# A graph-transformer layer on one core: one fp32 product fewer in front, lookup rows loaded by GpSimd, and the last messages moved ahead of the numerators and FFN transposes

## The chip, the cores and the metric

The kernel runs on one core of a Trainium2 chip. Its time is the device time in microseconds (us) of a whole launch; the median of several runs is compared. One further execution is profiled, and all durations of single instructions come from it. The engines are TensorE (PE, with its weight loads PEld), VectorE (DVE), ScalarE (ACT), GpSimd (POOL) and SyncE (SP). DMAs can be issued from SP, ACT and POOL.

## The reference

The input is a table `x` of N = 1250 nodes with D = 1024 features, and 20000 edges with source, destination and one of R = 8 relation types. With `xn = layernorm(x)`:

```
u   = xn @ root + bias + sum over r of mean over edges of type r into the node (xn[src]) @ weight[r]
z   = concat(u, xn) @ w_gate + b_gate
gnn = tanh(u) * z + xn * (1 - z)
mix = second-order Taylor linear attention of rms_norm(xn), 8 heads of 16, then @ w_out
x1  = x + gnn + mix
out = x1 + ffn(layernorm(x1))       # gate and up 1024 -> 352, silu, down 352 -> 1024,
                                    # weights and activations rounded to fp4 by blocks of 16
```

All inputs and outputs are float32.

## The kernel before, in words

Nodes are cut into ten blocks of up to 128 rows, and D into two column halves of 512. The kernel computes `y[r] = xn @ weight[r]` for all relations to DRAM (`y_d`, one array for each half), then gathers one row of it for every edge, weights it, and sums the rows by destination.

**Front.** LayerNorm (L186 to L200) takes each block: statistics on DVE, a square root on ACT, `normalize` (L125, L126) on DVE, a square with a sum on ACT (L194), eight transposes on PE (`transpose_cols`, L156), and two evacuations of the transposed tiles to `xnT`. `evac` (L84 to L90) gives evacuations in turn to ACT and DVE when `turns[0]` is 1, and to one engine alone when it is 0. Beside it a counting sort of the edges by destination runs: 16 steps build one-hot rows on DVE and counts on PE; tables are made of them; then 32 chunks of 5 x 125 edges (L307 to L336) look the tables up. A chunk loads the destinations of its 625 edges, the same row for all 128 partitions (`db`), takes the low seven bits (`lb`, L313), compares with the partition number (`lT`, L315, the weights of 20 small matmuls, L325 and L327), builds masks (L231), reduces the products (L328, L330), and counts equal destinations before each edge (`eq`, L333, five times). The pool of these tiles has two buffers. When all is known (L354), GpSimd scatters the 160 sorted columns of edge records to DRAM (`sort_d`, L363). PE's other work in the front is `plain(r)` (L369 to L390): fp32 products of half 0 for the first PLAIN = 4 relations, 80 matmuls of 128x128 by 128x512 each. Beside the last of them `x_limbs` (L403 to L416) splits `xnT` into three fp32r parts.

**Limb products.** The remaining products are made of three matmuls on the parts (L522 to L524): 240 matmuls for each. First come the R - PLAIN = 4 others of half 0, with 22 pieces of FFN weight quantisation on DVE spread among them (`ffn_rows`, to DRAM as `fgu_d` and `fdn_d`); then the eight of half 1, with the messages of half 0 among them; then five (queries and keys, root, gate of `x`) with 140 (EARLY) messages of half 1. A message (`gather` L437, `segments` L446 to L456) is 128 gathered rows, a selection matrix, two fp32r parts, two matmuls, a copy and a store to `seg_d`. LAG = 2 messages are gathered ahead, and GpSimd issues the gathers.

**Tail.** A list `rest` (L782 to L786) holds the attention sums, the preparation of open segments, `open_segments(0)`, ten `mix_pairs` (sums of key-value products), and FFN weight tiles to transpose (`ffn_weight`: load by SP, transposes, evacuations to `wguT` and `wdT`), with five numerators (`mix_num`, FIRST = 5) between them. The messages that are left, 19 calls, are spread over all of it but its last AFTER = 8 items. After the last message `open_segments(1)` (L756 to L771) loads the last row of each tile of `seg_d`, multiplies by selection matrices and adds the sums to `seg_d` by an indirect DMA from GpSimd (L769). SP loads the gate weights `wg` (4 MB) and `wo` at the end. Then ten blocks finish the layer (L810 to L892): a block gathers its segment sums (`ag`, L822), adds the root product to `u` (L828), transposes it, and makes the gate products (L836) and the FFN (L861, L877).

The order in which each engine carries out its instructions is fixed when the program is built, by a scheduler that knows the dependencies and estimates of durations; `issue_after` holds an instruction behind another one. A buffer of a pool is given again when its last reader is done, and memory of a closed pool is used again by later tiles, which then wait.

Of the kernel before, what the change touches and what calls it, by code (L numbers as in the profile page):

```python
# [8 lines left out]
F32 = mybir.dt.float32  # L9
F32R = mybir.dt.float32r  # L10
BF = mybir.dt.bfloat16
I32 = mybir.dt.int32
AF = mybir.ActivationFunctionType
ALU = mybir.AluOpType
# [4 lines left out]
N, D, R, E, I = 1250, 1024, 8, 20000, 352  # L19
NB, BR = 10, 128  # L20
KC = D // 128
# [4 lines left out]
MORE = 4096  # L26
H, DH = 8, 16
FIRST = 5
AFTER = 8
LAG = 2  # L30
EARLY = 140
PLAIN = 4
TOP = -4096
LOW = 2.0 ** -12
EXPONENT = 0x7F800000
# [13 lines left out]
def gps_layer(ctx: ExitStack, tc: tile.TileContext, x, src, dst, et, w_rel, w_root, bias,  # L49
# [19 lines left out]
    fgu_d = dram.tile([2 * I, D], F32, name="fgu_d")  # L69
    fdn_d = dram.tile([D, I], F32, name="fdn_d")  # L70
    seg_d = [dram.tile([ZERO + 1 + ST, HD], F32, name=f"seg{i}_d") for i in range(2)]
    sort_d = dram.tile([128 * ST, 4], F32, name="sort_d")

    def mm_tile():
# [10 lines left out]
    def evac(o, i):  # L85
# [3 lines left out]
        else:  # L89
# [8 lines left out]
    pidx = const.tile([128, 1], F32, name="pidx")  # L98
    G.iota(pidx, pattern=[[0, 1]], base=0, channel_multiplier=1,
           allow_small_or_imprecise_dtypes=True)  # L100
    eps = const.tile([128, 1], F32, name="eps")
    V.memset(eps, 1e-5)
    hdiff = const.tile([128, H], F32, name="hdiff")
# [21 lines left out]
    def normalize(o, xt, mr):  # L125
        V.tensor_scalar(o, xt, mr[:, 0:1], mr[:, 1:2], op0=ALU.subtract, op1=ALU.mult)  # L126
# [51 lines left out]
    with ExitStack() as front:  # L178
# [3 lines left out]
        xnT = xp.tile([128, KC, N], F32, name="xnT")  # L182


        with tc.tile_pool(name="ln", bufs=2) as ln:
            for b in range(NB):  # L186
                n = rows_of(b)
                xt = ln.tile([BR, D], F32, name="xt", bufs=8)[:n]
                nc.sync.dma_start(xt, x[block_rows(b), :])
                mr = stat[:n, b, :]  # L190
                mean_rstd(ln, mr, xt)
                normalize(xt, xt, mr)
                sq = ln.tile([BR, D], BF, name="sq", bufs=1)[:n]
                S.activation(sq, xt, AF.Square, accum_out=rms[:n, b, 0:1])  # L194
                transpose_cols(xnT, xt, n, D_CHUNKS, b * BR)
            V.tensor_scalar(rms[:, :, 0], rms[:, :, 0], 1e-24, None, op0=ALU.max)
            S.activation(rms[:, :, 0], rms[:, :, 0], AF.Sqrt)
            V.reciprocal(rms[:, :, 0], rms[:, :, 0])
            V.tensor_scalar(rms[:, :, 0], rms[:, :, 0], float(D) ** 0.5, None, op0=ALU.mult)
            V.tensor_scalar(rms[:, :, 1], rms[:, :, 0], float(DH) ** -0.5, None, op0=ALU.mult)  # L200


        with (tc.tile_pool(name="so", bufs=1, side="right") as so,
              tc.tile_pool(name="sc", bufs=2, side="right") as sc):
# [5 lines left out]
            hi_i = so.tile([80, 2, EP], I32, name="hi_i")  # L210
            V.tensor_scalar(lo_i, raw["dst"], 127, None, op0=ALU.bitwise_and)
            V.tensor_scalar(hi_i, raw["dst"], 7, None, op0=ALU.logical_shift_right)
            fl = so.tile([80, 5, 2, EP], F32, name="fl")
            V.tensor_copy(fl[:, 0], lo_i)
            V.tensor_copy(fl[:, 1], hi_i)
# [90 lines left out]
            LT = 5  # L306
            for c in range(ET // LT):  # L307
                t0 = c * LT
                db = sc.tile([128, LT * EP], I32, name="db")
                nc.sync.dma_start(db, bass.AP(tensor=dst.tensor, offset=dst.offset + t0 * EP,  # L310
                                              ap=[[0, 128], [1, LT * EP]]))
                lb = sc.tile([128, LT * EP], I32, name="lb")
                V.tensor_scalar(lb, db, 127, None, op0=ALU.bitwise_and)  # L313
                lT = sc.tile([128, LT * EP], BF, name="lT")
                V.tensor_scalar(lT, lb, pidx, None, op0=ALU.is_equal)  # L315
                msk = sc.tile([EP, LT, 2 * NHI + NHI * R], F32, name="msk")
# [336 lines left out]
    def mix_transposed(b):  # L653
        num = nums.pop(b)
        pt = tr_tile()
        n = rows_of(b)
        T.transpose(pt[:, 0, :n], num.rearrange("p h e -> p (h e)"), ident[:n, :n])
        S.copy(mixT[:, block_rows(b)], pt[:, 0, :n])

    with ExitStack() as late:  # L660
        op = late.enter_context(tc.tile_pool(name="op", bufs=1))
        pb = late.enter_context(tc.tile_pool(name="pb", bufs=8))
        kv = op.tile([BR, NB, 257], F32, name="kv")
        V.memset(kv[:, :, 256:257], 1.0)

# [105 lines left out]
                    in_=osum[:n, :], in_offset=None, compute_op=ALU.add)  # L771

        def ffn_weight(src, r0, n, c0, wide, o, chunks, col):
            wt = rawp.tile([128, HD], F32, name="raw")
            nc.sync.dma_start(wt[:n, :wide], src[r0:r0 + n, c0:c0 + wide])
            transpose_cols(o[:, c0 // 128:, :], wt, n, chunks, col)

# [1 line left out]
                   for i in range(2) for r0, n in I_CHUNKS for c0 in (0, HD)]  # L779
        down = [lambda a=(fdn_d, r0, n, 0, I, wdT, I_CHUNKS, r0): ffn_weight(*a) for r0, n in D_CHUNKS]  # L780
        rest = [mix_sums, open_rows, lambda: open_segments(0)]
        rest += [lambda b=b: mix_pairs(b) for b in range(NB)] + gate_up[:4]  # L782
        for b in range(FIRST):
            rest.append(lambda b=b: (mix_num(b), mix_transposed(b - 1) if b else None))
        rest += gate_up[4:] + down
        done = EARLY  # L786
        for i, p in enumerate(rest):
            p()
            while done < ST + LAG and (done - EARLY) * (len(rest) - AFTER) < (i + 1) * (ST + LAG - EARLY):
                message(1, done)  # L790
                done += 1
                if done == ST + LAG:
                    open_segments(1)
        for k in range(0, KC, 2):
            nc.sync.dma_start(wg[:, k:k + 2, :], w_gate[k * 128:(k + 2) * 128, :].rearrange("(k p) n -> p k n", p=128))
        nc.sync.dma_start(wo, w_out)
    late_r.close()
    mid.close()
# [121 lines left out]
```

## Time and profile before

| what | us |
|---|---|
| median of 3 runs (lowest, highest) | 2032.33 (2029.03, 2034.07) |
| the profiled execution, time | 2034.48 |
| the profiled execution, span of the core | 2032.7 |
| PE busy in the span | 1916.1 |
| DVE busy | 1319.7 |
| ACT busy | 736.0 |
| POOL busy | 569.5 |
| first limb product of half 0 starts | 352 |
| first gather of a message | 607 |
| last matmul of the last limb product ends | 1508.5 |

The mean TensorE clock granted in the span was 0.959 of full speed. In the profile a row of a group gives the line, the engine, the operation, the tiles with their shapes and the count, then busy time and mean nanoseconds of one, then the idle time of the engine just before and what ended it. A row of the timeline gives the start in us from the start of the span, the duration, the engine and the operation, and in brackets the idle time before it with what ended it. An fp32 matmul shows as two records, an fp32r one as one. The modelled end of a matmul can overlap the next one's start, so the count and the length of a full stretch tell more than the mean.

### The profile page before, as it was taken

How to read it: one execution, taken by the hardware profiler on the slowest of the kernel's cores; microseconds unless marked ns; L12 is line 12 of the kernel's file. 1: busy time of each engine (PE TensorE's matmuls, PEld its weight loads, DVE VectorE, ACT ScalarE, POOL GpSimd, SP SyncE). 2: the span in 40 equal slices, each digit the busy share in tenths (PEclk: the TensorE clock that was granted, in tenths of full speed). 3: DMA queues.
4: the chain of work that ended last, by engine and by line, in shares of the span. 5: the costliest groups of instructions: out<-in, count | busy, mean ns of one | idle time of the engine just before them, and what ended most of it. 6: DMA issues, size and time to landing. Idle time of an engine off the chain costs nothing. (4 is left out here: it accounts for less than half of the span.)

```text
span 2032.7 us, 23764 instructions
## 1 busy us (share of the span) xinstructions
PE 1916.1 (94%) x7748; PEld 1266.7 (62%) x7748; DVE 1319.7 (65%) x2947; ACT 736.0 (36%) x1279; POOL 569.5 (28%) x519
## 2 busy tenths in 40 slices
PE   8999999999999999999999989989889959999998
PEld 4465544777777777777777867767663324454544
DVE  9989840677765555455655675765667737777665
ACT  4111241111125554454554455555553123232311
POOL 1000177885003333233233234323234120010000
PEclk9999999999999999999999989999888559999999
DMA  5233222444337666667776678777788242122100
GB/s 207 70 109 121 86 68 51 132 120 125 121 127 240 223 223 222 221 221 230 228 224 208 204 248 258 243 237 252 235 285 314 76 137 85 63 83 68 37 21 29
DMA packets 159345, 327.81 MB, mean 161 GB/s; under 512 B 26414, under 2 KB 35284, under 8 KB 159222
## 3 DMA queue, kind: packets, MB, share of 16 engines
q10 hardware_dynamic: 76570, 141.23, 18.8%
q0 software_dynamic: 33952, 91.27, 17.3%
q1 hardware_dynamic: 48700, 93.79, 14.5%
q8 instruction: 61, 1.00, 0.2%
q14 instruction: 62, 0.51, 0.1%
HBM read 179.54 MB, written 146.49 MB: 160 GB/s over the span
## 5 line engine op out<-in xcount | busy, mean ns | idle before, releaser
L522 PE MATMUL ab<-wH,xH 128*128 128x512 f32 (+3 forms) x1360 | 536.9, 395 | 3.0 <-ACT wH L481 2.8
L524 PE MATMUL ab<-wD,xD 128*128 128x512 f32 (+3 forms) x1360 | 530.6, 396 | 6.1 <-DVE wD L483 5.6
L523 PE MATMUL ab<-wL,xL 128*128 128x512 f32 (+3 forms) x1360 | 533.3, 393 | 0.1
L437 POOL DMA_INDIRECT msg<-y_d,key x314 | 327.5, 1043 | 682.8 <-PE sm L454 402.1
L450 DVE SCALAR_TENSOR_TENSOR msg<-msg,weight,hi 128x512 fp32r<-128x512 f32 x314 | 234.1, 749 | 139.0 <-ACT hi L448 132.1
L524 PEld LDWEIGHTS ab<-wD,xD 128*128 128x128 f32 (+1 forms) x1360 | 253.2, 187 | 77.4 <-DVE wD L483 17.5
L522 PEld LDWEIGHTS ab<-wH,xH 128*128 128x128 f32 (+1 forms) x1360 | 255.3, 188 | 61.8 <-ACT wH L481 5.4
L523 PEld LDWEIGHTS ab<-wL,xL 128*128 128x128 f32 (+1 forms) x1360 | 254.8, 187 | 60.7 <-DVE wL L482 1.2
L381 PE MATMUL mm<-wt,xnT 128*128 128x512 f32 (+1 forms) x640 | 292.2, 601 | 0.0
L363 POOL DMA_INDIRECT sort_d<-pay,row x160 | 202.7, 1267 | 281.2 <-DVE pay L354 232.7
L448 ACT ACTIVATE hi<-msg,weight 128x512 fp32r<-128x512 f32 x314 | 221.8, 721 | 104.5 <-DMA msg<-y_d,key 38.5
L455 ACT COPY seg<-sm 128x512 f32<-128x512 f32 x314 | 181.7, 584 | 192.4 <-PE sm L454 157.7
L530 ACT ACTIVATE yt<-ab 128x512 f32<-128x512 f32 (+3 forms) x170 | 100.1, 592 | 272.2 <-PE ab L523 253.8
L531 DVE SCALAR_TENSOR_TENSOR yt<-ab,yt 128x512 f32<-128x512 f32 (+3 forms) x170 | 114.9, 679 | 124.7 <-ACT yt L530 119.5
L381 PEld LDWEIGHTS mm<-wt,xnT 128*128 128x128 f32 (+1 forms) x640 | 114.6, 188 | 119.8 <-issue 118.8
L446 DVE TENSOR_SCALAR sel<-iota_n,last_row 128x128 fp32r<-128x128 f32 x314 | 89.1, 286 | 108.5 <-PE sm L454 108.3
L453 PE MATMUL sm<-hi,sel 128*128 128x512 f32 x314 | 134.9, 433 | 25.9 <-ACT hi L448 19.6
L454 PE MATMUL sm<-msg,sel 128*128 128x512 f32 x314 | 137.0, 436 | 22.7 <-DVE msg L450 22.4
L836 PE MATMUL mm<-wg,uT 128*128 128x512 f32 (+1 forms) x320 | 142.5, 598 | 1.5 <-DVE mr L121 1.0
L482 DVE TENSOR_TENSOR wL<-raw,h 128x512 fp32r<-128x512 f32 x136 | 92.8, 682 | 70.9 <-PE mm L381 70.9
L481 ACT CAST wH<-h 128x512 fp32r<-128x512 f32 x136 | 83.6, 621 | 129.6 <-DVE h L480 117.2
L836 PEld LDWEIGHTS mm<-wg,uT 128*128 128x128 f32 (+1 forms) x320 | 59.9, 190 | 75.8 <-issue 71.2
(263 smaller groups left out, 2032.0 us busy)
## 6 DMA issues: line engine op xcount, KB each, us to landing
seg_d<-seg ACTq DMA_DIRECT2D x314, 256.0 KB
y_d<-yt ACTq DMA_DIRECT2D x144, 256.0 KB
raw<-in_L_gnn_weight_dram SPq DMA_DIRECT2D x96, 256.0 KB
db<-in_dst_dram SPq DMA_DIRECT2D x32, 312.5 KB
xt<-in_x_dram SPq DMA_DIRECT2D x18, 512.0 KB
wt<-in_L_gnn_weight_dram SPq DMA_DIRECT2D x24, 256.0 KB
msg<-y_d,key POOLq DMA_INDIRECT x314, 4.6
root_d<-yt ACTq DMA_DIRECT2D x18, 256.0 KB
```

The source lines that it names most:

```text
L363: st = G.indirect_dma_start(out=sort_d[:, :], out_offset=bass.IndirectOffsetOnAxis(ap=row[:, t:t + 1], axis=0), in_=pay[:, t, :], in_offse ...
L381: T.matmul(ps[:n], xnT[:, k, block_rows(b)], held[k], start=(k == 0), stop=(k == KC - 1))
L437: gathered_last[0] = G.indirect_dma_start(out=msg[:, :], out_offset=None, in_=y_d[nh][:, :], in_offset=bass.IndirectOffsetOnAxis(ap=key[:, ...
L448: S.mul(hi, msg, weight[:, t:t + 1])
L450: V.scalar_tensor_tensor(lo, msg, weight[:, t:t + 1], hi.bitcast(F32), op0=ALU.mult, op1=ALU.subtract)
L453: T.matmul(ps, sel, hi, start=True, stop=False)
L454: T.matmul(ps, sel, lo, start=False, stop=True)
L455: S.copy(seg, ps)
L522: T.matmul(pa[:p, :n], xH[:, k, ns], Wh[:, :n], start=(k == 0), stop=False)
L523: T.matmul(pa[:p, :n], xL[:, k, ns], Wl[:, :n], start=False, stop=(k == KC - 1))
L524: T.matmul(pb[:p, :n], xD[:, k, ns], Wd[:, :n], start=(k == 0), stop=(k == KC - 1))
L836: T.matmul(ps[:n], uT[:, k, :n], wg[:, k, cs], start=(k == 0), stop=(k == KC - 1))
```

## The change

1. PLAIN is 3 instead of 4: three fp32 products in front, five limb products of half 0 behind.
2. LayerNorm's normalisation goes to ACT (an Identity pass with a scale, and a bias `shift` that DVE makes, one column per block), and all LayerNorm evacuations go to ACT. After it evacuations alternate again.
3. The low bits of the destinations are written once to DRAM as bf16 (`lo_d`). Each lookup chunk loads `db` on 125 partitions instead of 128 and `lb` from `lo_d` on 128, both from GpSimd's queue; the DVE instruction that made `lb` is gone, and `lT` is made from bf16.
4. FFN weight tiles have a pool of their own with six buffers (`fw`) instead of the three of the limb weights.
5. All remaining messages are spread over the sums, open segments and pairs alone; `open_segments(1)` follows directly. Then come five numerators, each followed by four of the 20 FFN weight tiles.
6. GpSimd loads `wg`, held behind its last gather, instead of SP.

```diff
--- before.py
+++ after.py
@@ -26,10 +26,9 @@
 MORE = 4096
 H, DH = 8, 16
 FIRST = 5
-AFTER = 8
 LAG = 2
 EARLY = 140
-PLAIN = 4
+PLAIN = 3
 TOP = -4096
 LOW = 2.0 ** -12
 EXPONENT = 0x7F800000
@@ -69,6 +68,7 @@
     fgu_d = dram.tile([2 * I, D], F32, name="fgu_d")
     fdn_d = dram.tile([D, I], F32, name="fdn_d")
     seg_d = [dram.tile([ZERO + 1 + ST, HD], F32, name=f"seg{i}_d") for i in range(2)]
+    lo_d = dram.tile([1, E], BF, name="lo_d")
     sort_d = dram.tile([128 * ST, 4], F32, name="sort_d")
 
     def mm_tile():
@@ -98,6 +98,7 @@
     pidx = const.tile([128, 1], F32, name="pidx")
     G.iota(pidx, pattern=[[0, 1]], base=0, channel_multiplier=1,
            allow_small_or_imprecise_dtypes=True)
+    shift = const.tile([BR, NB], F32, name="shift")
     eps = const.tile([128, 1], F32, name="eps")
     V.memset(eps, 1e-5)
     hdiff = const.tile([128, H], F32, name="hdiff")
@@ -182,6 +183,7 @@
         xnT = xp.tile([128, KC, N], F32, name="xnT")
 
 
+        turn[0], turns[0] = 1, 0
         with tc.tile_pool(name="ln", bufs=2) as ln:
             for b in range(NB):
                 n = rows_of(b)
@@ -189,7 +191,8 @@
                 nc.sync.dma_start(xt, x[block_rows(b), :])
                 mr = stat[:n, b, :]
                 mean_rstd(ln, mr, xt)
-                normalize(xt, xt, mr)
+                V.scalar_tensor_tensor(shift[:n, b:b + 1], mr[:, 0:1], -1.0, mr[:, 1:2], op0=ALU.mult, op1=ALU.mult)
+                S.activation(xt, xt, AF.Identity, bias=shift[:n, b:b + 1], scale=mr[:, 1:2])
                 sq = ln.tile([BR, D], BF, name="sq", bufs=1)[:n]
                 S.activation(sq, xt, AF.Square, accum_out=rms[:n, b, 0:1])
                 transpose_cols(xnT, xt, n, D_CHUNKS, b * BR)
@@ -199,6 +202,7 @@
             V.tensor_scalar(rms[:, :, 0], rms[:, :, 0], float(D) ** 0.5, None, op0=ALU.mult)
             V.tensor_scalar(rms[:, :, 1], rms[:, :, 0], float(DH) ** -0.5, None, op0=ALU.mult)
 
+        turns[0] = 1
 
         with (tc.tile_pool(name="so", bufs=1, side="right") as so,
               tc.tile_pool(name="sc", bufs=2, side="right") as sc):
@@ -210,6 +214,9 @@
             hi_i = so.tile([80, 2, EP], I32, name="hi_i")
             V.tensor_scalar(lo_i, raw["dst"], 127, None, op0=ALU.bitwise_and)
             V.tensor_scalar(hi_i, raw["dst"], 7, None, op0=ALU.logical_shift_right)
+            lo_b = so.tile([80, 2, EP], BF, name="lo_b")
+            V.tensor_copy(lo_b, lo_i)
+            G.dma_start(lo_d.rearrange("o (a b c) -> b (o a) c", a=2, b=80), lo_b)
             fl = so.tile([80, 5, 2, EP], F32, name="fl")
             V.tensor_copy(fl[:, 0], lo_i)
             V.tensor_copy(fl[:, 1], hi_i)
@@ -306,11 +313,11 @@
             LT = 5
             for c in range(ET // LT):
                 t0 = c * LT
-                db = sc.tile([128, LT * EP], I32, name="db")
-                nc.sync.dma_start(db, bass.AP(tensor=dst.tensor, offset=dst.offset + t0 * EP,
-                                              ap=[[0, 128], [1, LT * EP]]))
-                lb = sc.tile([128, LT * EP], I32, name="lb")
-                V.tensor_scalar(lb, db, 127, None, op0=ALU.bitwise_and)
+                db = sc.tile([EP, LT * EP], I32, name="db")
+                G.dma_start(db, bass.AP(tensor=dst.tensor, offset=dst.offset + t0 * EP,
+                                       ap=[[0, EP], [1, LT * EP]]))
+                lb = sc.tile([128, LT * EP], BF, name="lb")
+                G.dma_start(lb, lo_d[:, t0 * EP:(t0 + LT) * EP].to_broadcast([128, LT * EP]))
                 lT = sc.tile([128, LT * EP], BF, name="lT")
                 V.tensor_scalar(lT, lb, pidx, None, op0=ALU.is_equal)
                 msk = sc.tile([EP, LT, 2 * NHI + NHI * R], F32, name="msk")
@@ -660,6 +667,7 @@
     with ExitStack() as late:
         op = late.enter_context(tc.tile_pool(name="op", bufs=1))
         pb = late.enter_context(tc.tile_pool(name="pb", bufs=8))
+        fw = late.enter_context(tc.tile_pool(name="fw", bufs=6))
         kv = op.tile([BR, NB, 257], F32, name="kv")
         V.memset(kv[:, :, 256:257], 1.0)
 
@@ -771,7 +779,7 @@
                     in_=osum[:n, :], in_offset=None, compute_op=ALU.add)
 
         def ffn_weight(src, r0, n, c0, wide, o, chunks, col):
-            wt = rawp.tile([128, HD], F32, name="raw")
+            wt = fw.tile([128, HD], F32, name="fw")
             nc.sync.dma_start(wt[:n, :wide], src[r0:r0 + n, c0:c0 + wide])
             transpose_cols(o[:, c0 // 128:, :], wt, n, chunks, col)
 
@@ -779,20 +787,25 @@
                    for i in range(2) for r0, n in I_CHUNKS for c0 in (0, HD)]
         down = [lambda a=(fdn_d, r0, n, 0, I, wdT, I_CHUNKS, r0): ffn_weight(*a) for r0, n in D_CHUNKS]
         rest = [mix_sums, open_rows, lambda: open_segments(0)]
-        rest += [lambda b=b: mix_pairs(b) for b in range(NB)] + gate_up[:4]
-        for b in range(FIRST):
-            rest.append(lambda b=b: (mix_num(b), mix_transposed(b - 1) if b else None))
-        rest += gate_up[4:] + down
+        rest += [lambda b=b: mix_pairs(b) for b in range(NB)]
         done = EARLY
         for i, p in enumerate(rest):
             p()
-            while done < ST + LAG and (done - EARLY) * (len(rest) - AFTER) < (i + 1) * (ST + LAG - EARLY):
+            while done < ST + LAG and (done - EARLY) * len(rest) < (i + 1) * (ST + LAG - EARLY):
                 message(1, done)
                 done += 1
-                if done == ST + LAG:
-                    open_segments(1)
-        for k in range(0, KC, 2):
-            nc.sync.dma_start(wg[:, k:k + 2, :], w_gate[k * 128:(k + 2) * 128, :].rearrange("(k p) n -> p k n", p=128))
+        open_segments(1)
+
+        with tc.issue_after(gathered_last[0]):
+            for k in range(0, KC, 2):
+                G.dma_start(wg[:, k:k + 2, :], w_gate[k * 128:(k + 2) * 128, :].rearrange("(k p) n -> p k n", p=128))
+        weights = gate_up + down
+        for b in range(FIRST):
+            mix_num(b)
+            if b:
+                mix_transposed(b - 1)
+            for p in weights[len(weights) * b // FIRST:len(weights) * (b + 1) // FIRST]:
+                p()
         nc.sync.dma_start(wo, w_out)
     late_r.close()
     mid.close()
```

## The prediction

> **What bounds the kernel now.** The sections with busy totals and with tenths of the span come first: TensorE is busy nearly everywhere, so only its thin places and its own work can give time.
>
> ```profile
> PE 1916.1 (94%) x7748; PEld 1266.7 (62%) x7748; DVE 1319.7 (65%) x2947; ACT 736.0 (36%) x1279; POOL 569.5 (28%) x519
> ...
> PE   8999999999999999999999989989889959999998
> PEclk9999999999999999999999989999888559999999
> ```
>
> The one thin place is slice 33 (a 5, with a granted clock of 5 in it and before it). Then I cut the span at the joints: end of the one-hots, end of the lookups, first limb product, first message, last limb matmul, last pair, last numerator, and the first transpose of `u` in the ten final blocks.
>
> ```profile
> 0.00:101.40 101.40, 91.46 (x566) 49.45 (x567) 94.49 (x260) 29.25 (x69) 7.79 (x20) 1.00 0.41 138
> 101.40:236.40 135.00, 133.52 (x860) 77.53 (x860) 121.04 (x506) 15.01 (x44) 0.00 (x0) 1.00 0.36 116
> 236.40:352.00 115.60, 114.42 (x269) 49.65 (x268) 41.59 (x95) 34.10 (x67) 87.01 (x72) 1.00 0.21 50
> 352.00:587.10 235.10, 228.33 (x960) 176.05 (x961) 162.70 (x331) 43.43 (x73) 115.69 (x89) 1.00 0.42 122
> 587.10:1508.70 921.60, 880.26 (x3695) 686.53 (x3694) 551.76 (x1097) 474.37 (x806) 296.47 (x292) 0.98 0.72 230
> 1508.70:1574.50 65.80, 54.84 (x194) 22.87 (x193) 48.22 (x115) 23.52 (x42) 29.20 (x18) 0.82 0.92 325
> 1574.50:1621.90 47.40, 45.47 (x82) 15.18 (x81) 34.66 (x82) 8.53 (x18) 5.70 (x6) 0.50 0.22 69
> 1621.90:1669.20 47.30, 21.34 (x84) 11.85 (x83) 17.35 (x46) 13.35 (x26) 8.99 (x7) 0.61 0.42 116
> 1669.20:2032.70 363.50, 346.43 (x1047) 177.57 (x1047) 247.85 (x420) 94.46 (x138) 18.61 (x16) 0.98 0.18 60
> ```
>
> After the times each line gives busy PE, weight loads, DVE, ACT, POOL, then clock, DMA share and GB/s. PE is full in all but the eighth, where it works 21.34 of 47.30. The timeline there says why:
>
> ```profile
> 1635.76 0.78 PE L454 MATMUL sm<-msg,sel 128*128 128x512 f32 x1
> ...
> 1644.79 1.91 PE L766 MATMUL mm<-s,osel 29*29 29x512 f32 x2 [1.35 <-DMA s<-seg_d]
> ...
> 1652.82 2.12 POOL L769 DMA_INDIRECT seg_d<-osum,orow  x1 [5.36 <-ACT mixT L658]
> ...
> 1662.96 1.03 POOL L822 DMA_INDIRECT ag<-seg_d,node_at  x1 [8.02 <-DVE xf L807]
> ...
> 1667.94 1.23 DVE L828 TENSOR_TENSOR u<-rt,ag 128x1024 f32<-128x1024 f32 x1 [2.40 <-DMA ag<-seg_d,node_at]
> 1669.22 1.11 PE L156 MATMUL tr<-ident,u 128*128 128x128 f32 x4 [17.34 <-DVE u L828]
> ```
>
> The last message of half 1 is multiplied at 1635.8, late, because the messages are spread over numerators and FFN transposes. Behind it come its store, the reload, the open-segment sums, their adds to DRAM, the gathers, `u`: 33.5 us, of which PE is idle for the last 17.3. So the tail is a chain begun late, and the front is PE work.
>
> **The change, front.** One product leaves the fp32 form and becomes a limb product. fp32: 164 records in the 70.0 us from 260 to 330, where PE does nothing else, 0.427 each; a product is 80 matmuls of two records, 160 x 0.427 = 68.3 us. Limb: the fourth window holds four, 235.1 / 4 = 58.8 (two later ones between their last blocks take 60.1 and 55.9). PE work alone: 58.8 - 68.3 = **-9.5 us**, if the front stays full with a quarter of its filler gone.
>
> LayerNorm: ten normalisations of 0.80 us (L126) go from DVE to ACT, and with them half of the evacuations (0.68 on DVE, 0.58 on ACT). ACT then has per block 0.29 square root, about 1.25 for the new pass (the square of the same shape takes 1.06, with 0.19 for its accumulator), 1.25 for the square itself and 2 x 0.58: about 3.9, 39 us in all instead of DVE's. LayerNorm ends near 45 instead of 34. PE has 18 filler matmuls placed there and waits somewhat, and the one-hots, DVE-bound, catch up because DVE loses about 15 us there. I count nothing, between -5 and +10.
>
> Lookups: 32 chunks lose `lb` (0.48, L313, 15.3 us in all) on DVE and get a `lT` from bf16 (0.55 before; a gain of up to 0.25 is not counted). DVE's chunk falls from 4.1 us of work at a cadence of 4.65 to about 3.6. The changed order puts 84 fp32 matmuls (0.854 each) and 640 small ones (0.058 in this stage) between the first lookup and the last: 72 + 37 = 109 us, 3.4 per chunk. So lookups want 3.6 per chunk, 115 us, against 135 now. After them 88 fp32 matmuls, 75 us, cover the limbs of x (DVE 243 to 280, 36 us now). Uncovered, those would cost up to 36; they are covered. The first limb product starts at 352 - 68.3 = 283.7 when PE is full; I take 285.
>
> What the lookups get instead is two loads per chunk on POOL's queue where SP had one. `db` (double buffered) for chunk c+2 waits for `eq` of chunk c, and `lb` sits behind it on POOL. A turn is issue 0.3 + landing + the 2.6 of DVE work from landing to last `eq`, and two buffers share it. No row shows this load issued from POOL. From below: `sp` (314 KB, 128 rows, issued at 602.98, its reader at 606.03) lands in 3.05 us; turn 5.95, 3.0 per chunk, free. From above: `wt` at the start, 9.6 us, but as eight issues at once; turn 12.5, 6.25 per chunk. Same bytes and one at a time speak for the `sp` end. [...]
>
> The sort's 160 scatters (L363, 1.48 apart, 237 us) start about 30 us earlier and still end before the messages. FFN quantisation spreads over five products. **Front: 285 + 5 x 58.5 = 577.5 against 587.1, -9**, from -25 (limb products at 55.9) to +25.
>
> **The middle**, 587 to 1508.7, is unchanged: 0.
>
> **The change, tail.** All 27 messages left after the last limb matmul lie among sums and pairs (L437 waits 66.3 us in 18 places for PE's L454 in the tail, so spacing, not gathering, sets them). Now eight or so of them are done by 1574.5 beyond sums and pairs; packed at the 2.95 us that they keep there from 1508 to 1556, 27 take 80 us if nothing is gained, about 1588; with pairs between them and without the 4 MB of `wg` on the queues (issued at 1522.9 to 1527; DMA share 0.92 in that window, 325 GB/s), some 75: **1583**.
>
> Behind them PE runs five numerators and 20 FFN groups. Numerators: 43.6 us from 1574.5 to 1618 with five messages in it (1.4 of PE each, 7): 7.3 each, 36.5 at clock 0.50. Groups: 16 in 21 us from 1622 to 1643, and four more in small gaps: I take 18 for 20, being dense without messages. 36.5 + 18 = 54.5: **1638**. The segment chain of 33.5 us less its last gather and `u` starts at 1583 and ends its adds near 1610, +5 for `wg`, which now loads from POOL behind the last gather; so it hides under the 54.5. The gather of block 0 then waits only for the last transpose, since `ag` reuses memory of the FFN tiles: 6.3 us, beneath the sixth numerator (7.3) that PE has in front of `u`. So `u` is transposed near **1646 against 1669.2: -23**. Without the numerator as cover it is 1652, -17. `wg` (4 MB at about 325 GB/s, 13 us, and POOL's issues of about a microsecond each) is in by 1610 and has 35 us to spare. SP loses it and only gains. The last 363.5 us remain.
>
> Sum: -9 - 23 = -32. On the profiled 2034.48 (span 2032.7 and 1.8 around it) that is 2002; on the median 2032.33, **2000**.
>
> **Rivals.**
> *The loads of the lookups (slower).* If `db` lands like the burst at the start, 9.6 us, the cadence is 6.25 where PE has fill for about 3.8: 30 x 2.4 = 72 us of stalled PE, as its order is fixed; 2000 + 72 = about 2070. It decides from (L + 2.9)/2 = 4.9, a landing of 6.9 us: there all of -32 is eaten. [...] Against: `sp` in 3.05 and a share of only 0.36 in that stage. 0.2.
> *The front gives nothing* (ACT holds LayerNorm, cadence 4.0): only the tail, 2009. 0.25, near the forecast.
> *The tail is held by DMA or the half clock.* From 1510 to 1560 the queues are near full; with `wg` gone to the end and the messages dense, they may come no closer than 2.95, and the gathers among back-to-back pair products took 4.3 and 5.3 us. Messages end at 1600, tail -6; with the front about 2018. 0.2.
> *Both in full*, limb products at 55.9 and messages 2.4 apart: -24 and -38, 1970. 0.1.
> The forecast's own neighbourhood has the rest, 0.25. A measurement of this kernel can tell about 0.3%, 6 us. Slower by more: 0.2; within: 0.1, from the borders of the loads and the tail; faster: 0.7. The range goes from 1972 to 2038.
>
> **What would show it.** Right: `db` landing under 5.5 us and PE full from 100 to 285; first limb matmul near 285, first gather near 597; last L454 near 1583; adds to `seg_d` over before the last FFN transpose; no idle PE over 3 us before the transpose of `u` at about 1646 less the 9 of the front. Wrong: waits of DVE for `db` or `lT`, LayerNorm past 55, L454 after 1600 or PE waiting for `ag` again.

## The result, and the profile after

Before 2032.33 us (median of 5 runs, 2029.03 to 2037.19), after 2018.26 (2014.05 to 2023.47): a ratio of 0.9931, 95% interval 0.9907 to 0.9955. So 14 us were won where 32 were forecast. The profiled execution was the fastest of the five: 2014.05, span 2012.3 against 2032.7, so the stages below differ by 20 us and not by 14. The page's slices:

```profile
PE 1889.7 (94%) x7828; PEld 1281.7 (64%) x7828; DVE 1315.7 (65%) x2940; ACT 755.3 (38%) x1307; POOL 614.1 (31%) x588
...
PE   6999999999999999999999989999897689999998
...
PEclk8999999999999999999999989889998759999999
```

PE is thin at the start (a 6, clock 8) where it was an 8 with clock 9, and slices 31 and 32 are a 7 and a 6. The span is cut at the same joints as before (columns as in the prediction), with the start cut finer:

```profile
0.00:16.60 16.60, 3.91 (x16) 3.14 (x16) 7.51 (x28) 8.72 (x15) 5.37 (x16) 1.00 0.90 273
16.60:60.00 43.40, 36.32 (x219) 21.39 (x220) 33.66 (x116) 29.09 (x56) 8.16 (x15) 0.88 0.58 176
60.00:97.30 37.30, 35.98 (x285) 18.39 (x284) 34.93 (x93) 4.91 (x15) 1.59 (x3) 1.00 0.14 48
97.30:110.00 12.70, 12.48 (x30) 5.59 (x31) 12.30 (x60) 1.17 (x2) 1.06 (x2) 1.00 0.37 109
110.00:221.30 111.30, 111.23 (x809) 68.31 (x809) 98.49 (x428) 13.08 (x41) 26.78 (x49) 1.00 0.55 142
221.30:298.20 76.90, 75.71 (x179) 32.49 (x177) 42.08 (x99) 30.48 (x61) 55.79 (x46) 1.00 0.23 57
298.20:583.80 285.60, 282.50 (x1201) 221.23 (x1202) 191.96 (x384) 55.06 (x93) 153.27 (x116) 1.00 0.42 120
583.80:1502.40 918.60, 879.77 (x3696) 688.17 (x3694) 544.50 (x1078) 473.97 (x805) 300.63 (x291) 0.97 0.72 229
1502.40:1568.00 65.60, 46.53 (x159) 21.06 (x159) 38.52 (x99) 24.97 (x43) 22.77 (x21) 0.79 0.87 300
1568.00:1603.00 35.00, 23.08 (x74) 7.06 (x73) 26.63 (x50) 10.12 (x18) 12.94 (x9) 0.82 0.67 235
1603.00:1652.10 49.10, 39.16 (x125) 19.30 (x124) 35.65 (x87) 9.25 (x24) 7.73 (x6) 0.50 0.26 66
1652.10:2012.30 360.20, 343.03 (x1047) 175.55 (x1047) 249.45 (x427) 94.46 (x138) 17.98 (x16) 0.99 0.18 60
```

The first limb product starts at 298.2, and not at 285; PE lost time before 60 and was full in the lookups. The last block of the last limb product of half 0 starts at 578.2 against 581.6 (-3.4), and all limb products end at 1502.5 against 1508.9 (-6.4); the first transpose of `u` is at 1652.1 against 1669.2 (-17.1), and the end comes 20.4 earlier. GpSimd's timeline shows what happened at the start:

```profile
3.12 0.63 POOL L212 DMA_DIRECT2D raw_et<-in_edge_type_dram  x1
3.72 1.12 POOL L317 DMA_DIRECT2D db<-in_dst_dram  x2
4.82 1.13 POOL L384 DMA_DIRECT2D wt<-in_L_gnn_weight_dram  x2
20.09 0.65 POOL L219 DMA_DIRECT2D lo_d<-lo_b  x1 [14.14 <-DVE stat L122]
20.73 1.62 POOL L384 DMA_DIRECT2D wt<-in_L_gnn_weight_dram  x3
27.15 1.06 POOL L320 DMA_DIRECT2D lb<-lo_d  x2 [4.80 <-DMA lo_d<-lo_b]
28.20 1.59 POOL L384 DMA_DIRECT2D wt<-in_L_gnn_weight_dram  x3
```

Six of the eight weight tiles of the first fp32 product stand behind the new store of the low bits, which waits for DVE. In the kernel before, all were issued by 10.7:

```profile
3.71 2.74 POOL L377 DMA_DIRECT2D wt<-in_L_gnn_weight_dram  x5
...
9.79 0.84 POOL L377 DMA_DIRECT2D wt<-in_L_gnn_weight_dram  x1 [0.50 <-DMA raw_et<-in_edge_type_dram]
```

PE pays for it in the changed kernel:

```profile
16.64 3.71 PE L388 MATMUL mm<-wt,xnT 128*128 128x512 f32 x4 [1.15 <-DMA wt<-in_L_gnn_weight_dram]
22.82 1.30 PE L157 MATMUL tr<-ident,xt 128*128 128x128 f32 x8 [2.47 <-ACT xt L195]
...
28.39 2.08 PE L388 MATMUL mm<-wt,xnT 128*128 128x512 f32 x2 [3.93 <-DMA wt<-in_L_gnn_weight_dram]
```

And the tail, PE's timeline:

```profile
1587.66 0.40 PE L461 MATMUL sm<-msg,sel 128*128 128x512 f32 x1
...
1602.80 1.90 PE L774 MATMUL mm<-s,osel 29*29 29x512 f32 x2 [9.22 <-DMA s<-seg_d]
...
1652.12 1.94 PE L157 MATMUL tr<-ident,u 128*128 128x128 f32 x8 [2.47 <-issue]
```

The old idle time of 17.3 us before `u` is now 2.5, but 9.2 us stand earlier: the second matmul of the open segments sits on PE inside the second numerator, and numerators and transposes are queued behind it.

### The profile page after: what moved, and what is told of

Its sections match the earlier page's. It is cut to its first block, busy times and chain, and to the rows that moved or that the text cites. A ratio compares the mean times of both kernels' runs of the same rounds, so it can differ in the third digit from the quotient of the medians.

```text
span 2012.3 us, 24046 instructions
## 1 busy us (share of the span) xinstructions
PE 1889.7 (94%) x7828; PEld 1281.7 (64%) x7828; DVE 1315.7 (65%) x2940; ACT 755.3 (38%) x1307; POOL 614.1 (31%) x588
## 3 DMA queue, kind: packets, MB, share of 16 engines
q8 instruction: 62, 1.02, 0.2%
## 5 line engine op out<-in xcount | busy, mean ns | idle before, releaser
L529 PE MATMUL ab<-wH,xH 128*128 128x512 f32 (+2 forms) x1440 | 569.2, 395 | 2.3 <-ACT wH L488 2.3
L531 PE MATMUL ab<-wD,xD 128*128 128x512 f32 (+2 forms) x1440 | 562.9, 395 | 3.8 <-DVE wD L490 3.1
L530 PE MATMUL ab<-wL,xL 128*128 128x512 f32 (+2 forms) x1440 | 565.3, 393 | 0.0
L531 PEld LDWEIGHTS ab<-wD,xD 128*128 128x128 f32 (+1 forms) x1440 | 268.6, 187 | 76.9 <-DVE wD L490 12.8
L529 PEld LDWEIGHTS ab<-wH,xH 128*128 128x128 f32 (+1 forms) x1440 | 270.2, 188 | 64.8 <-ACT wH L488 4.1
L530 PEld LDWEIGHTS ab<-wL,xL 128*128 128x128 f32 (+1 forms) x1440 | 270.1, 188 | 64.4 <-DVE wL L489 0.4
L388 PE MATMUL mm<-wt,xnT 128*128 128x512 f32 (+1 forms) x480 | 225.6, 611 | 5.1 <-DMA wt<-in_L_gnn_weight_dram 5.1
L537 ACT ACTIVATE yt<-ab 128x512 f32<-128x512 f32 (+2 forms) x180 | 106.0, 592 | 319.8 <-PE ab L530 308.0
L538 DVE SCALAR_TENSOR_TENSOR yt<-ab,yt 128x512 f32<-128x512 f32 (+2 forms) x180 | 121.5, 680 | 144.8 <-ACT yt L537 143.9
L388 PEld LDWEIGHTS mm<-wt,xnT 128*128 128x128 f32 (+1 forms) x480 | 85.7, 190 | 90.0 <-issue 82.5
```

The lines of the kernel that those rows point to most:

```text
L388: T.matmul(ps[:n], xnT[:, k, block_rows(b)], held[k], start=(k == 0), stop=(k == KC - 1))
L529: T.matmul(pa[:p, :n], xH[:, k, ns], Wh[:, :n], start=(k == 0), stop=False)
L530: T.matmul(pa[:p, :n], xL[:, k, ns], Wl[:, :n], start=False, stop=(k == KC - 1))
L531: T.matmul(pb[:p, :n], xD[:, k, ns], Wd[:, :n], start=(k == 0), stop=(k == KC - 1))
```

## The experiments

Theory after the result: the front gave away its saving at PE's start (weights late, LayerNorm from ACT), and the tail was held by late messages and by one wait on PE. Rivals stand in each expectation. A ratio compares with runs of the kernel before that were made beside it. The stage marks come from each kernel's one profile, in us: the start of the first limb product, the end of the last limb matmul, the time from there to the first transpose of `u`, and PE busy in the first 60 us.

| kernel | ratio to before (95%) | first limb | limbs end | to `u` | busy in 60 |
|---|---|---|---|---|---|
| before | 1 | 352.0 | 1508.9 | 160.4 | 50.5 |
| changed | 0.9931 (0.9907 to 0.9955) | 298.2 | 1502.5 | 149.7 | 40.2 |
| front_only | 0.9959 (0.9941 to 0.9978) | 296.6 | 1509.5 | 157.9 | 42.2 |
| tail_only | 0.9942 (0.9921 to 0.9964) | 352.9 | 1514.2 | 149.6 | 49.5 |
| plain3_only | 0.9908 (0.9885 to 0.9930) | 283.9 | 1484.1 | 155.5 | 49.8 |
| wt_first | 0.9913 (0.9883 to 0.9942) | 295.4 | 1505.6 | 150.0 | 41.7 |
| wt_mid | 0.9923 (0.9900 to 0.9946) | 290.8 | 1495.3 | 146.9 | 46.7 |
| ln_dve | 0.9876 (0.9850 to 0.9902) | 288.3 | 1492.5 | 149.8 | 46.8 |
| db_sp | 0.9843 (0.9797 to 0.9888) | 287.1 | 1489.0 | 146.2 | 46.9 |
| old_front3 | 0.9845 (0.9826 to 0.9863) | 284.3 | 1486.3 | 147.8 | 48.7 |
| seg_late | 0.9898 (0.9872 to 0.9923) | 296.3 | 1503.5 | 140.2 | 42.4 |
| msg_bufs | 0.9895 (0.9862 to 0.9929) | 298.3 | 1503.3 | 136.7 | 40.8 |
| loads_late | 0.9893 (0.9853 to 0.9934) | 296.4 | 1503.5 | 142.6 | 42.7 |
| wg_late | 0.9900 (0.9873 to 0.9927) | 297.0 | 1507.0 | 141.3 | 40.7 |
| best_loads_sp | 0.9823 (0.9798 to 0.9849) | 287.3 | 1493.6 | 136.5 | 46.2 |
| best | 0.9813 (0.9787 to 0.9840) | 287.1 | 1485.8 | 136.2 | 46.1 |
| best_old_front3 | 0.9737 (0.9719 to 0.9754) | 282.5 | 1482.6 | 129.3 | 50.1 |

The middle, from the last limb product of half 0 to the last of all, has the same work in all of them and took 911 to 925 us. A single profile's span is therefore good to some 7 us, and I judge by the marks of a stage. How far these scatter is seen where kernels share a stage. The six with the changed front have their first limb product at 296.3 to 298.3, the three with the front of `db_sp` at 287.1 to 287.3, the three with the old front and three products at 282.5 to 284.3. The seven with the changed tail need 146.2 to 150.0 to `u`, the three with the old one 155.5 to 160.4. By the ratios alone, front_only, tail_only, plain3_only, wt_first, wt_mid, seg_late, msg_bufs, loads_late and wg_late are not apart from the changed kernel, since the intervals overlap; what is said of them rests on the marks.

**Front and tail apart.** front_only has the changed front with the old `rest`; tail_only is before with the lines from `ffn_weight` to the end of the list changed.

> The changed kernel with the tail of before (messages spread over numerators and FFN transposes, wg by SP, FFN tiles in the old pool); front and LayerNorm changes kept. Additive theory, from the changed kernel's profile: the last limb matmul ends 6 us earlier than before (1502 against 1508.5) and the tail is worth nothing, so a span of 2026 to 2028 and a ratio of 0.996 to 0.998. Rival, the two parts interact (POOL's and SP's queues or the granted clock carry over): the last limb matmul ends at 1508 or 1495, or the tail moves by over 4 us.

> The kernel before with the new tail alone. Additive theory: limb matmuls end at 1508.5 as before, the first transpose of u comes 150 us later (149.7 in the changed kernel) instead of 160.5, so 11 to 14 us are won and the ratio is 0.993 to 0.995. Rival, interaction: the tail wins over 18 or under 6.

The parts add up within their intervals (0.9959 x 0.9942 = 0.9901 against 0.9931), and the tail takes 149.6 us with either front. The front's end fell in the scatter of the middle: 1509.5 is outside of what I expected, though its own marks to 579 are those of the changed kernel.

**The front's edits.** plain3_only is one number:

```diff
-PLAIN = 4
+PLAIN = 3
```

> The kernel before with three fp32 products in front instead of four, and nothing else. The prediction's arithmetic: an fp32 product of 68.3 us goes and a limb product of 57 (four steps of 56.8 in the changed kernel) comes, so 10 to 14 us are won if the sort on DVE stays covered: the last limb matmul ends at 1495 to 1499, ratio 0.993 to 0.995. Rival cover: without the fourth product PE waits for the sort and the parts of x; the first limb product starts 10 us or more late and the ratio is 0.998 or more.

It wins 19 us by the ratio, no less than the whole change (the intervals overlap), and to the end of the limb products 25 us where the change won 6. PE is full to the end of the front, and the limb products start 14 us before those of the changed kernel:

```profile
283.89 0.50 PE L522 MATMUL ab<-wH,xH 128*128 128x512 f32 x1 [2.71 <-ACT wH L481]
```

So LayerNorm on ACT and rows by GpSimd together cost 14 us. In both kernels PE has 1533 records up to its first limb product; it is busy for 275.6 of 298.2 us in the changed one and 269.9 of 283.9 here. Of the 14.3 us some 9 are idle time, therefore, and 6 are the same matmuls taking longer. wt_first issued the eight weight loads ahead of everything on GpSimd's queue:

```diff
+        for k in range(KC):
+            G.dma_start(ahead_w[k], w_rel[0, k * 128:(k + 1) * 128, :HD])
         with tc.tile_pool(name="ln", bufs=2) as ln:
...
-            held = []
+            held = list(ahead_w) if r == 0 else []
```

> The changed kernel, with the eight weight loads of the first fp32 product issued by GpSimd ahead of everything else of the sort. Theory queue: in the changed kernel six of these loads stand on GpSimd's queue behind the store of the low bits, which waits 14 us for DVE, and PE then runs dry and falls to the half clock; here PE idles 10 to 12 us in the first 60 instead of 20, the last block of the first limb product starts 8 to 12 us earlier than 351.0 and the ratio to before is 0.987 to 0.990. Rival LayerNorm: the transposes wait for the normalisation on ACT; the weights are there earlier but PE idles over 16 us in the first 60 and less than 4 us is won.

By its expectation the queue had lost: PE is busy for 41.7 of the 60 us. But the wait had only moved. GpSimd issued the eight weight loads at once and then waited for one of them to land before each further issue, so the edge data went out at 8.5 to 12.5 instead of 1.7 to 3.7 (what sets eight as the limit is not shown). PE waited for the edge data, with transposes behind it:

```profile
1.65 4.47 POOL L189 DMA_DIRECT2D wt<-in_L_gnn_weight_dram  x8
8.51 0.66 POOL L215 DMA_DIRECT2D raw_dst<-in_dst_dram  x1 [2.39 <-DMA wt<-in_L_gnn_weight_dram]
...
29.72 1.12 PE L238 MATMUL sm<-ident,fl 80*125 80x80 f32 x4 [3.68 <-DVE fl L224]
```

wt_mid puts the same eight loads behind the three of edge data:

```diff
                 G.dma_start(raw[name], a.rearrange("(a b c) -> b a c", a=2, b=80))
...
+            for k in range(KC):
+                G.dma_start(ahead_w[k], w_rel[0, k * 128:(k + 1) * 128, :HD])
```

> The changed kernel with the eight weight loads of the first fp32 product on GpSimd's queue behind the three loads of edge data and ahead of the store of the low bits; nothing else is changed, LayerNorm stays on ACT and the lookup rows on GpSimd. In the earlier try the weights stood ahead of the edge data, and the wait only moved: PE waited 3.7 us for the edge numbers, with transposes of LayerNorm queued behind. Theory queue, second try: PE is busy 45 to 48 of the first 60 us instead of 40.2, the last block of the first limb product starts at 338 to 343 instead of 351, and the ratio is 0.986 to 0.989. Rival LayerNorm on ACT (with lookup rows that compete): still under 43 us busy, 347 or later, ratio over 0.991.

Here PE is busy 46.7 of 60 and the limb products start 7.4 earlier, at 290.8: the order on GpSimd's queue explains about half of the 14.3 us lost against plain3_only. The ratio, 0.9923, is where the rival had put it. But PE's busy time is the theory's, and the gain at the first limb product is clear of the scatter of that mark. ln_dve and db_sp undo one edit each:

```diff
-        turn[0], turns[0] = 1, 0
...
-                V.scalar_tensor_tensor(shift[:n, b:b + 1], ...
-                S.activation(xt, xt, AF.Identity, ...
+                normalize(xt, xt, mr)
```

> The changed kernel with the normalisation of LayerNorm back on DVE and its evacuations in turn on both engines; lookup loads, three fp32 products and the tail as changed. Theory LayerNorm (after the weights loaded first had won nothing): ACT's normalisation, with a square root before it and a reciprocal and a shift on DVE between, delivers blocks late and in pairs, so that PE idles 20 us in the first 60 and runs part of it at the half clock; here PE idles 10 to 12 there, the transposes end near 35 instead of 53, the last block of the first limb product starts 8 to 12 us before 351.0, near 340, and the ratio is 0.988 to 0.991. Rival DVE: DVE has 15 us more to do before the lookups, the one-hots come later and PE has nothing else by then; under 3 us are won.

```diff
-            G.dma_start(lo_d.rearrange(...), lo_b)
...
-                G.dma_start(db, bass.AP(...))
-                G.dma_start(lb, lo_d[:, t0 * EP:(t0 + LT) * EP].to_broadcast([128, LT * EP]))
+                nc.sync.dma_start(db, bass.AP(...))
+                V.tensor_scalar(lb, db, 127, None, op0=ALU.bitwise_and)
```

> The changed kernel with the lookup rows as before: db by SP on 128 partitions, lb by DVE from it. The prediction's view: lookups paced by DVE, about 4.6 us per chunk instead of the 3.5 measured in the changed kernel (111.3 us for 32), of which PE's fp32 filler covers less now that there is a quarter less of it: the lookups take 130 to 140 us, fewer fp32 matmuls are left behind them and the first limb product starts within 5 us of the changed kernel's, ratio 0.991 to 0.996. Rival: the loads by GpSimd are what the front's gain hangs on, the first limb product starts 10 us or more later, ratio over 0.997.

Both start near 288, because in both all the weights are out early again, by 15.6 in ln_dve and by 11.0 in db_sp (in ln_dve the store of the low bits comes only at 34.7, behind them; in db_sp there is none). My expectation for db_sp was wrong: it said that going back to rows by SP wins nothing, and the kernel starts its limb products 11 us earlier, although the sort ends on DVE at 238.2 instead of 228.4. Nobody waits for that end: PE is busy for 225.2 of the 227.1 us from 60 to the first limb product. With both undone, old_front3 starts at 284.3.

> The changed kernel with LayerNorm and the lookup rows as in the kernel before: three fp32 products and the new tail alone. Theory cost: LayerNorm on ACT and lookup rows by GpSimd bring PE nothing and together cost 14 us at its start, so this kernel starts the first limb product near 284 as the one with three products alone, against 298.2 changed, ends its limb products near 1485, and has a ratio of 0.982 to 0.986, the product of the two parts measured alone. Rival: the new tail needs the earlier sort (rows sorted 14 us sooner) or the lighter queue of SP; then the limb products end at 1490 or later and the ratio is over 0.988.

The four corners: both edits 298.2 (290.8 with the queue mended), rows by GpSimd alone 288.3, LayerNorm on ACT alone 287.1, neither 284.3. LayerNorm on ACT costs 2.8 and rows by GpSimd 4.0, together about the 6.5 left in wt_mid; with both edits the weights are late as well, 7.4 more. Why each of the two costs its 3 to 4 us by itself is not shown. The ratio of old_front3, 0.9845, is the product of the parts (0.9908 x 0.9942 = 0.9851); the new tail needs neither.

**The tail's wait.** seg_late calls the second part of `open_segments(1)` after the third numerator:

```diff
-        open_segments(1)
+        second = open_segments(1, True)
...
             for p in weights[len(weights) * b // FIRST:len(weights) * (b + 1) // FIRST]:
                 p()
+            if b == 2:
+                second()
```

> The changed kernel, with the second half of the open segments of half 1 (its matmuls and its add) behind the third numerator on PE instead of inside the second. Theory wait: in the changed kernel PE stands 9.2 us at 1593 to 1603 for the reload of the last rows, with numerators and FFN transposes queued behind; here that idle time goes, the first transpose of u is 7 to 10 us earlier counted from the last limb matmul (140 to 143 instead of 149.7), ratio 0.988 to 0.990. Rival chain: the adds then come last and the gather of block 0 waits for them; under 3 us are won and PE waits before the transpose of u.

140.2, as the wait theory had it. The matmul has no wait left, and the second add, issued at 1616.7, has landed by 1626.2, before the gather of block 0, which waits until 1635.5 for the last FFN transpose:

```profile
1614.58 1.21 PE L774 MATMUL mm<-s,osel 29*29 29x512 f32 x2
...
1643.68 1.94 PE L157 MATMUL tr<-ident,u 128*128 128x128 f32 x8 [2.48 <-issue]
```

Why was the reload late at all? wg_late moves the gate weights only, with the same order on PE (`added[0]` is the last add to `seg_d`):

```diff
-        with tc.issue_after(gathered_last[0]):
+        with tc.issue_after(added[0]):
             for k in range(0, KC, 2):
                 G.dma_start(wg[...])
```

> The changed kernel with the four loads of the gate weights (4 MB) on GpSimd's queue behind the last add of open segments instead of behind the last gather; the order on PE is the same. Theory collision: in the changed kernel the gate weights, issued at 1580 to 1583, fill the queues just when the last messages are stored; the last copy waits 4.4 us for a store, its own store takes 6.0 us until the reload is issued (3.0 in the kernel before), and so PE stands 9.2 us. Here PE waits under 4 us at the second matmul of the open segments and the first transpose of u is 143 to 146 us behind the last limb matmul instead of 149.7, ratio 0.989 to 0.991. Rival chain: the store, the reload and the matmul take that long by themselves; PE still waits 7 us or more and nothing is won. A third way, the gate weights now late for the first block: a wait for wg before its gate products, slower than the changed kernel.

PE's wait shrinks to 1.7 us, and 8 us are won in the tail. In the changed kernel ACT's last copy waited 4.4 us for an earlier store to land:

```profile
1580.17 3.00 POOL L801 DMA_DIRECT2D wg<-in_L_gnn_w_gate_dram  x4
...
1591.65 0.58 ACT L462 COPY seg<-sm 128x512 f32<-128x512 f32 x1 [4.41 <-DMA seg_d<-seg]
1592.26 0.33 ACTq L463 DMA_DIRECT2D seg_d<-seg  x1
1598.28 0.24 SPq L769 DMA_DIRECT2D s<-seg_d  x1
```

With the gate weights held back it waits for PE alone, and the reload is issued 2.4 us after the last store (6.0 in the changed kernel):

```profile
1591.51 0.58 ACT L462 COPY seg<-sm 128x512 f32<-128x512 f32 x1 [2.68 <-PE sm L461]
1592.13 0.33 ACTq L463 DMA_DIRECT2D seg_d<-seg  x1
1594.53 0.24 SPq L771 DMA_DIRECT2D s<-seg_d  x1
1598.94 1.90 PE L776 MATMUL mm<-s,osel 29*29 29x512 f32 x2 [1.70 <-DMA s<-seg_d]
```

**The messages.** msg_bufs gathers every other message of the tail into `rawp`; loads_late issues the loads of blocks 0 and 1 and of `wo` by GpSimd behind the last gather.

```diff
-        msg = em.tile([128, HD], F32, name="msg")
+        if nh and t >= EARLY and t % 2:
+            msg = rawp.tile([128, HD], F32, name="raw")
+        else:
+            msg = em.tile([128, HD], F32, name="msg")
```

> The changed kernel, in which every other message of the tail is gathered into the three buffers that the limb weights have left, seven buffers in all instead of four. Theory buffers: in the changed kernel the 27 messages take 85 us (3.2 each) because a gather waits for a buffer (30 us in 13 places for the second matmul) and lands 4 to 7 us later; here the last message is 70 to 76 us behind the last limb matmul and the ratio is 0.988 to 0.990. Rival transfers: the queues are full with tail loads from 1502 to 1530 (share 0.87), gathers land late whatever the buffers: 82 to 86 us and the same time.

```diff
-        nc.sync.dma_start(wo, w_out)
+        with tc.issue_after(gathered_last[0]):
+            G.dma_start(wo, w_out)
...
         with tc.issue_after(gathered_last[0]):
+            Q = G if b < 2 else nc.sync
+            Q.dma_start(xt, x[rows, :])
+            Q.dma_start(rt, root_d[rows, :])
+            Q.dma_start(gx, gx_d[rows, :])
```

> The changed kernel, in which the loads of x, root product and gate product of the first two blocks and of the output projection (3.6 MB) are issued by GpSimd behind the last gather instead of by SP among the messages. Theory transfers: without them messages are gathered sooner, the last one 74 to 79 us behind the last limb matmul instead of 85; the time falls by 4 to 8 us, unless the loads then come late for block 0. Rival buffers: messages stay at 83 to 86 us, and the time within 3 us or, if the loads come late for the first block, later.

The last message comes 81.3 and 79.8 us behind the last limb matmul instead of 85.2: each is worth 4 to 5, and less than its theory had said (70 to 76, and 74 to 79). msg_bufs wins 9 more behind that, since its gathers end earlier, the gate weights go out at 1564 to 1570, ahead of the last stores, and PE's wait is 1.1.

> Three edits on the changed kernel together: lookup rows as before (SP and DVE), the second half of the open segments behind the third numerator, and seven message buffers in the tail. If they add up: last limb matmul at 1489, first transpose of u 132 to 137 us behind it, span 1981 to 1986, ratio 0.974 to 0.978. If the last two remove the same wait: 140 us behind it and a ratio near 0.980.

> The same three edits, and the loads of the first two blocks and of the output projection behind the last gather on GpSimd. If transfers and buffers are two separate limits of the messages: the last message 73 to 77 us behind the last limb matmul, and 3 to 5 us less than without this fourth edit. If they are one: no difference above 2 us, or a loss of up to 5 where the loads are now late for the first block.

> The same with the three edits of the tail (second half of the open segments behind the third numerator, seven message buffers, loads of the first two blocks behind the last gather). If LayerNorm on ACT still costs 3 us with lookup rows on SP, this kernel is 2 to 4 us faster than the one with all edits and LayerNorm on ACT (0.9813), ratio 0.978 to 0.981; if that cost was noise, they are equal.

With the buffers and without the late loads (best_loads_sp) the last message comes at 80.3, with both (best) at 79.9, where 73 to 77 had been expected; the two ratios are not apart. So the two gains do not add. best_loads_sp reached its 132 to 137 to `u`, but not its ratio of 0.974 to 0.978. What holds the messages at 80 is not settled; PE is busy for 65.4 of 80.2 us there in best, at a mean granted clock of 0.85. The last kernel, three fp32 products with the old LayerNorm and lookups and the tail's edits, is the fastest, 1978.0 us. It beats best by 15 us by the ratios and by 10 by the spans of the profiles, where 2 to 4 were expected. It is 7 us ahead at the last product of half 0 and wins 7 more in the tail (129.3 against 136.2), for which I have no cause.

## Why the prediction was wrong

- **One fp32 product fewer.** Right in kind, and mis-sized. The fp32 side came out: it said 283.7 for a full front, and plain3_only started at 283.9. The limb side was put at 58.8, the mean of the four products before. But five products need 278.6 us there to the last block, where four needed 229.6: the fifth adds 49.0. The first three distances between last blocks were 60.4, 60.0 and 55.9 before and are 59.1, 55.7 and 56.4 in plain3_only, so the other products got shorter beside it; the same FFN quantisation is spread over one more of them, which fits but was not tested alone. So the edit gives -19 to that point (562.5 against 581.6) where -9.5 was the sum.
- **"I count nothing, between -5 and +10".** This step of the front failed. The cost of LayerNorm on ACT by itself, 2.8, lay inside that margin. What was put at nothing is what the edits do together on GpSimd's queue: the prediction walked that queue for the lookups, and not for what stands on it before them, where the store of the low bits waits for DVE ahead of six weight tiles. Over a full front it allowed 1.3 us, and 14.5 were lost: 7.4 by the queue, the rest by LayerNorm on ACT and by the rows from GpSimd.
- **Lookups.** The pace was right: 111.3 us, 3.5 per chunk, PE full, beside a DVE that is busy for 98.5 of them. The new loads land between the two ends of the prediction (3.05 and 9.6), near the lower:

```profile
db<-in_dst_dram POOLq DMA_DIRECT2D x21, 305.2 KB, 3.9
lb<-lo_d POOLq DMA_DIRECT2D x28, 156.2 KB, 4.0
```

  `lb` often stands right behind `db`, so these medians do not tell what one load takes by itself. The packets of the trace do: those of one `db` load on 125 rows by GpSimd that ran alone, at 54.2, take 1.9 us from first to last, and those of the load on 128 rows by SP at 151.1 in the kernel before take 2.0. `lT` from bf16 takes 0.38 instead of 0.55: a gain of 0.17, where up to 0.25 was not counted. No run shows the 3.8 us per chunk that the slow rival's sum gives PE as fill, or the 4.0 per chunk in the rival of a front that gives nothing: the lookups went at 3.5 with PE busy for 111.23 of 111.30 us, and the slow rival did not come. But the gain in pace was worth nothing: DVE's end of the sort moved by 14 us, and PE did not wait for it in either case.
- **Front, -9, was measured -3.4** to the last limb product of half 0, by two errors of opposite sign: 13 us too little at the start, and 7 too much in the limb products (292.5 put, 285.6 taken).
- **Messages, 75 us, took 85.2.** This step of the tail failed in its size. The 2.95 us between messages cannot be found in the trace of the kernel before: the second matmuls of 14 messages start there from 1509.8 to 1555.6, 3.5 apart, at which 27 take 95. They came at 3.2, closer than before, but not at 2.8. Buffers and tail loads hold 4 to 6 of the 10 us.
- **"So it hides under the 54.5."** This step failed in its mechanism. The chain of the open segments was compared with the whole work behind it, but one of its links is a matmul on PE, and PE takes its work in the order that the scheduler fixed: it had put the matmul within the second numerator. And the +5 for the gate weights fell on the last store and the reload, just ahead of that matmul: PE waited 9.2 us, and 1.7 without that load. The work itself was put 8 too high, in part because four of the 20 weight tiles had been transposed among the messages (from 1534 to 1556); so the time from the last message to `u`, with the wait in it, came to 64.4 against a forecast of 63. That agreement is luck.
- **The tail, -23, was -10.7**: 10 for the messages, and a wait of 9.2 less the 8 that the work was cheaper. The last ten blocks took 360.2 against 363.5, which other kernels with the same tail show as scatter (363.4 in tail_only).
- **The rival of a tail held by DMA** named 2018, and that is what was measured. Its parts were not: it had the messages 91 us behind the limb products (85.2) and the front at -9 (-3.4).

## What to carry to other kernels

Where an edit puts a DMA on a queue, list what stands behind it on that queue from its first wait on, and not only in the stage that the edit is for: here a 39 KB store that waited 14.1 us for DVE made PE run dry, busy for 40.2 of the first 60 us where it was 46.7 with the weights ahead of that store. Work taken off an engine whose end nobody waits for bought nothing here (DVE's end of the sort came 14 us earlier, and PE did not wait for it), and the engine that gets it may be worse placed (LayerNorm on ACT cost 2.8 by itself). When a chain is to be hidden under an engine's work, look for a link of it on that engine: here one matmul held PE for 9.2 us. And when a 4 MB load is moved "to where there is room", see which stores and reloads of a chain it meets: with it held back that wait was 1.7.

## What had not been expected of the hardware

The stage between the last limb product of half 0 and the last of all differed by 14 us (911 to 925) between kernels that have the same work there. A 4 MB load issued among 256 KB stores put a wait of 4.4 us for a store's landing into ACT, and 6.0 us between the last store's issue and the reload, where it was 2.4 with the load held back. The granted clock alone did not tell here how fast matmuls ran after waits. Behind PE's waits of 2 to 4 us in the first 30 us of the changed kernel two records of an fp32 matmul took 2.08 us, and later 1.02; the granted clock is 0.88 from 16.6 to 60, and 0.50 from 24 to 30. In front_only the same pair took 2.08 and the granted clock is 1.00:

```profile
33.95 1.02 PE L388 MATMUL mm<-wt,xnT 128*128 128x512 f32 x2
...
27.27 2.08 PE L389 MATMUL mm<-wt,xnT 128*128 128x512 f32 x2 [3.36 <-DMA wt<-in_L_gnn_weight_dram]
...
16.60:60.00 43.40, 37.78 (x231) 22.21 (x231) 34.31 (x114) 29.08 (x57) 8.16 (x15) 1.00 0.56 170
```

The first row is of the changed kernel, the other two are of front_only, whose limb products start at 296.6: the lower granted clock of the changed kernel's start is worth no more than the 2 us by which the two differ.
